# Scatters, masks, roots and zero fills rearranged, and an earlier shared expert, in an attention-plus-experts kernel

## The chip, the core and the metric

The kernel runs on one core of a Trainium2 chip. The metric is the device time of one launch in microseconds (us). Five engines run their own instruction queues in order: PE (matrix multiply; PEld is its weight load), DVE and ACT (elementwise work, ACT with function tables), POOL (elementwise work and indirect DMA) and SP (here only DMA issue). They wait for each other through semaphores. Sixteen DMA engines carry all transfers.

## What is computed

Sixteen sequences of 512 tokens, 128 wide, all float32. First a linear attention with a rotary-like expansion of q and k, then a mixture of experts, each followed by a layernorm:

```python
q, k, v = silu(x @ Wq), silu(x @ Wk), x @ Wv            # 16 heads of 8
q, k = lrpe(q, theta), lrpe(k, theta)                   # [t * cos(theta * n), t * sin(theta * n)]
out = ((q @ k.T) * causal) @ v                          # no softmax
out = (out @ Wo) * sigmoid(x @ G1 @ G2)
x = layernorm(x + layernorm(out) * gamma + beta)

xn = x * rsqrt(mean(x * x) + eps)
probs = softmax(xn @ router_w.T)                        # 8 experts, top 2 per token
dispatch, valid = first 1280 tokens of each expert, which of these slots are filled
routed = scatter_add(w * valid * (silu(x[dispatch] @ rg) * (x[dispatch] @ ru)) @ rd)
shared = (silu(x @ sg) * (x @ su)) @ sd                 # width 1024, for every token
x = layernorm(x + shared + routed)
```

## The kernel before

There are three stages. PE has work in all of them, and the order of PE, ACT, DVE and POOL is written out by hand (`tc.manual_schedule(engines=ORDERED)`, line 18 names the four). SP is not among these: the scheduler may place SP's DMA issues elsewhere than the program text has them, as soon as what they read is there.

**Attention, lines 177 to 780.** Work goes in turns `t` from -2 to 64, one tile of 128 tokens per turn, four tiles (`NC`) per sequence, in a pipeline: in turn `t` `project(t + 2)` computes q, k, v and the gate (`pq`, ACT evacuates it, DVE makes `hat` from it and the table `cst_tok` of cosines and sines), `turn_over(t + 1)` transposes, `energies(t)` multiplies q and k and DVE masks the result (`et`, four of 128x384), `values(t - 1)` multiplies with v (`pout`) and `remember` keeps a running state for the next tile. When a sequence's four tiles are done, the generator `after(b)` is appended to `turns`: output projection (`po`), two layernorms (`ln_stats`, `rstd_of`, `w`), the normalised rows `x1`, their transposes (`px`, `x1T`) and the router's logits. Each call of `advance(turns)` takes one of its steps, two calls per turn; a step that yields "narrow" waits for the call with that name. `route(b0, b1)` does top-2, the ranks of tokens in their expert and `count` per expert, some steps per turn (`sprinkle`). The resulting row numbers feed `scatter`: an indirect DMA on POOL that writes 128 token rows of `R` = 132 numbers into `xg_dram`, two per turn (`scatter_behind`, at the end of a turn), 128 in all.

**Shared expert.** Its steps for all sequences stand in one list, `feed`: per sequence eight `gate_half` (`pg`, L125) and eight `up_half` (`pu`, L133), then eight `down_half` (`pd`, L143). `shared(t)` takes one step where PE would have room: two per turn once the sequence is `ready`, one per turn of the loop that follows turn 64 (lines 780 to 797, which runs until the last scatter and twelve steps more), and what is left after the experts, where it covers the final layernorms.

**Experts, lines 800 to 951.** For each of eight experts the weights and the 1280 gathered rows `xg` (128 partitions x 10 x 132) are loaded, the rows transposed in three parts of 512, 512 and 256 (`turn_rows`: `ept`, copied to `xgT`), multiplied (`peg`, `peu`, `eh`, `ped`) and scattered by an indirect DMA into `y_dram`, two rows per token. The transposes of expert e+1 are done within expert e: after each `eh` of its second part first one `back` (`ped`), then one part of `turn_rows`.

**End, lines 953 to 983.** `load_pair` reads the two routed rows of each token back, `add_up` adds them, `finish_lot` does the last layernorm for lots of four tiles (single tiles for the last sequence) and stores them. A generator of these moves one step per step of `feed`.

Two fills belong to the change. `y_dram` must be zero where no expert writes a row; `zero` (128x2048) is written to it by eight DMAs of 1024 KB. Empty slots of `xg_dram` must be recognised; `empty`, with `NOBODY` as its token number, is written there by eight DMAs of 660 KB, before any scatter. `fill(t)` issues one per turn in turns 0 to 15.

At the start `cst_tok` is made from theta: broadcast to 128 partitions by its load (`th_sb`), multiplied by the positions, reduced by 2 pi in three steps (`C1`, `C2`, `C3`), then sines on ACT. Chunk 0 is done first and chunks 1 to 3 together, all before turn -2's `hat`. POOL clears the padded v tiles (`vpad`, `vlow`) and makes the masks and routing constants.

Of the kernel before, what the change touches and what calls it, by code (L numbers as in the profile page):

```python
# [10 lines left out]
F32 = mybir.dt.float32  # L11
I32 = mybir.dt.int32
# [7 lines left out]
P = 128  # L20
# [8 lines left out]
NOBODY = 1.0e6  # L29
# [6 lines left out]
C1 = 6.28125  # L36
C2 = 2029.0 / 2 ** 20
C3 = 2.0 * math.pi - C1 - C2
# [9 lines left out]
def tile_kernel(  # L48
# [37 lines left out]
    nc.gpsimd.memset(neghalf, -0.5)  # L86
    x1 = keep.tile([P, NT, R], F32, name="x1")
# [5 lines left out]
    idx = keep.tile([P, 2, NT], I32, name="idx")  # L93
    sg_sb = keep.tile([P, IS], F32, name="sg_sb")
# [10 lines left out]
    def rstd_of(var, n, eps):  # L105
        ve = small.tile([P, n], F32, tag="ve", name="ve")
        nc.vector.tensor_scalar(ve, var, eps, None, ALU.add)  # L107
        r = small.tile([P, n], F32, tag="rstd", name="rstd")
        nc.gpsimd.tensor_tensor(r, ve, neghalf[:, :n], ALU.pow)  # L109
        return r  # L110


    def shared_steps(b):
# [6 lines left out]
        def gate_half(i):  # L120
            if i % half == 0:
                h[i // half] = hp.tile([P, half, N], F32, tag="h", name=f"h_{b}_{i}")
            pool, tag = home["g"]
            pg = pool.tile([P, N], F32, tag=tag, name=f"pg_{b}_{i}")
            nc.tensor.matmul(pg, sg_sb[:, ts(i, P)], seq, start=True, stop=True)  # L125
            sl = sp.tile([P, N], F32, tag="sl", name=f"sl_{b}_{i}")
            nc.scalar.activation(sl, pg, AF.Silu)  # L127
            h["s", i] = sl

# [30 lines left out]
    done = set()  # L160
    latest = [None]
# [15 lines left out]
    with ExitStack() as ph:  # L177
# [21 lines left out]
        with tc.manual_schedule(engines=ORDERED):  # L199
            th_sb = cst.tile([P, D + HALF], F32, name="th_sb")  # L200
            nc.sync.dma_start(th_sb, theta.partition_broadcast(P))
# [3 lines left out]
            load_xT(0)  # L205
            g1t_sb = cst.tile([8, D], F32, name="g1t_sb")
            nc.scalar.dma_start(g1t_sb, g1t)
            g2_sb = cst.tile([8, D], F32, name="g2_sb")
            nc.scalar.dma_start(g2_sb, g2)
# [7 lines left out]
            nc.gpsimd.memset(rw_sb, 0.0)  # L217
# [3 lines left out]
            load_x(1)  # L221
# [3 lines left out]
            nc.sync.dma_start(bet, beta.partition_broadcast(P))  # L225

# [19 lines left out]
            expi = cst.tile([P, E], I32, name="expi")  # L246
            nc.gpsimd.iota(expi, pattern=[[1, E]], base=0, channel_multiplier=0)
            expf = cst.tile([P, E], F32, name="expf")
            nc.vector.tensor_copy(expf, expi)
            first = cst.tile([P, E], F32, name="first")  # L250
            nc.vector.tensor_scalar(first, expf, -1.0, float(E), ALU.mult, ALU.add)
            startrow = cst.tile([P, E], F32, name="startrow")
            nc.vector.tensor_scalar(startrow, expf, float(CAP), float(-NSLOT), ALU.mult, ALU.add)
            count = cst.tile([P, E], F32, name="count")
            nc.vector.memset(count, 0.0)
            goes_on = {}
            for n in sorted({(b1 - b0) * NC for b0, b1 in groups}):
                goes_on[n] = cst.tile([P, E, n + 1], F32, name=f"goes_on{n}")
                nc.gpsimd.memset(goes_on[n], 1.0)
                nc.gpsimd.memset(goes_on[n][:, :, 0], 0.0)  # L260


            ones = cst.tile([P, P], F32, name="ones")
            nc.vector.memset(ones, 1.0)

            causal = cst.tile([P, 3, HALF], F32, name="causal")
            nc.gpsimd.memset(causal, 1.0)
            for block, at in ((0, 0), (0, HALF), (1, HALF), (2, 0)):
                rows = causal[at : at + HALF, block, :]
                nc.gpsimd.affine_select(  # L270
                    rows, rows, pattern=[[1, HALF]], compare_op=ALU.is_ge, fill=0.0, base=0, channel_multiplier=-1
                )
            tri = cst.tile([P, P], F32, name="tri")
            nc.gpsimd.affine_select(
                tri, ones, pattern=[[1, P]], compare_op=ALU.is_gt, fill=0.0, base=0, channel_multiplier=-1
            )
# [7 lines left out]
            )  # L284


            NVP = 4
            vpads = []
            for i in range(NVP):
                vp = cst.tile([P, 4, 4, 40], F32, name=f"vpad{i}")  # L290
                nc.gpsimd.memset(vp, 0.0)

                vl = cst.tile([P, 8, 40], F32, name=f"vlow{i}")
                nc.gpsimd.memset(vl, 0.0)
                vpads.append((vp, vl))


            toki = cst.tile([P, NT], I32, name="toki")
            nc.gpsimd.iota(toki, pattern=[[P, NT]], base=0, channel_multiplier=1)
            zero = hp.tile([P, 4 * N], F32, tag="h", name="zero")  # L300
            nc.gpsimd.memset(zero, 0.0)
            empty = hp.tile([P, NS, R], F32, tag="h", name="empty")
            nc.gpsimd.memset(empty, 0.0)
            nc.gpsimd.memset(empty[:, :, D], NOBODY)


            pg = ps_w.tile([P, D], F32, tag="w", name="pg12")
            nc.tensor.matmul(pg, g1t_sb, g2_sb, start=True, stop=True)

            cst_tok = cst.tile([P, NC, 2, 16, 2, 8], F32, name="cst_tok")
            scratch = hp.tile([P, 2, NC, D + HALF], F32, tag="h", name="scratch")
            ang, turns_ = scratch[:, 0], scratch[:, 1]
            for c0, c1 in ((0, 1), (1, NC)):
                a, k = ang[:, c0:c1, :], turns_[:, c0:c1, :]
                for c in range(c0, c1):
                    nc.vector.tensor_scalar(ang[:, c, 0:D], th_sb[:, 0:D], pos[:, 0, c : c + 1], None, ALU.mult)
                    nc.vector.tensor_scalar(ang[:, c, D:], th_sb[:, D:], pos[:, 1, c : c + 1], None, ALU.mult)
                nc.vector.tensor_scalar(k, a, 1.0 / (2.0 * math.pi), MAGIC, ALU.mult, ALU.add)  # L320
                nc.vector.tensor_scalar(k, k, MAGIC, None, ALU.subtract)
                for part in (C1, C2, C3):
                    nc.vector.scalar_tensor_tensor(a, k, -part, a, ALU.mult, ALU.add)
                nc.vector.tensor_scalar(a, a, -PI_BELOW, PI_BELOW, ALU.max, ALU.min)
                nc.vector.scalar_tensor_tensor(k, a, -1.0, a, ALU.mult, ALU.max)

                for c in range(c0, c1):
                    for s, (from_, scale, bias) in enumerate([(turns_, -1.0, half_pi), (ang, 1.0, 0.0)]):
                        for to, n0, n1 in ((cst_tok[:, c, 0], 0, D), (cst_tok[:, c, 1, 1::2], D, D + HALF)):
                            nc.scalar.activation(  # L330
                                to[:, :, s, :], from_[:, c, n0:n1].rearrange("p (h d) -> p h d", d=8), AF.Sin,
                                scale=scale, bias=bias,
                            )
                if c0 == 0:
                    nc.vector.tensor_copy(  # L335
                        W[:, 0:384].rearrange("p (h n) -> p h n", n=24)[:, :, 8:16], pg.rearrange("p (h d) -> p h d", d=8)
                    )
            for c0, c1 in ((0, 1), (1, NC)):
                nc.vector.tensor_copy(
                    cst_tok[:, c0:c1, 1, 0::2].rearrange("p c h s d -> p c h (s d)"),  # L340
                    cst_tok[:, c0:c1, 0, 0::2].rearrange("p c h s d -> p c h (s d)"),
                )
            nc.vector.tensor_scalar(wo_sb, wo_sb, 0.5, None, ALU.mult)
            nc.vector.tensor_copy(x1[:, :, D], toki)


        y_rows = y_dram.rearrange("(p q r) d -> p q (r d)", p=P, r=4 * N // D)
        x_rows = xg_dram.rearrange("(p q r) d -> p q (r d)", p=P, r=NS)

        def fill(i):  # L350
            if i < 8:
                nc.sync.dma_start(y_rows[:, i, :], zero)
            elif i < 16:
                nc.sync.dma_start(x_rows[:, i - 8, :], empty.rearrange("p r d -> p (r d)"))

        hats, qkt, ets, states, gates, oTs = {}, {}, {}, {}, {}, {}


        def project(t):
# [22 lines left out]
            for i in range(2):  # L382
                mine = slice(HALF * i, HALF * i + HALF)
                nc.scalar.copy(vl[mine, :, 8 * i : 8 * i + 8], pq[mine, 8:16, 16 + 8 * i : 24 + 8 * i])
            hats[t] = hat = wk2.tile([P, 2, 2 * D], F32, tag="hat", name=f"hat_{t}")
# [350 lines left out]
        with tc.manual_schedule(engines=ORDERED):  # L736
            for t in range(-2, NT + 1):
                coming, here, left = 0 <= t + 2 < NT, 0 <= t < NT, 0 <= t - 1 < NT
                stopped("wait")
                if coming:  # L740
# [3 lines left out]
                    project(t + 2)  # L744
                if t == 2:
# [3 lines left out]
                if 0 <= t < 16:  # L749
                    fill(t)  # L750
# [5 lines left out]
                advance(turns)  # L756
# [272 lines left out]
```

## Time and profile before

| | |
|---|---|
| Median of 11 runs | 889.5 us (887.49 to 890.67, and one of 2649.25) |
| The profiled execution's own time | 889.07 us |
| Its span, first to last instruction | 887.4 us |
| PE busy in the span | 827.0 us (93%) |
| DVE, ACT, POOL busy | 556.5, 441.2, 345.1 us |
| Mean granted PE clock | 0.983 |
| DMA moved | 62.97 MB, of it 31.88 MB written to HBM |

The rest of the page is in 40 slices of 22.2 us, a digit is the busy share in tenths:

```profile
## 2 busy tenths in 40 slices
PE   2898999999989999998999999999999999999990
PEld 1576667666855866765666666777667676666670
DVE  7678788998888888978533343333333326875543
ACT  3767777677676767654322233333333333343332
POOL 4023222156755665477666413343333340110101
PEclk9999999999999999999999999999999999999995
DMA  8941111012111110000000422332211005631001
```

The first eighteen or so slices are attention, with DVE nearly as full as PE; the next five the loop that follows turn 64; the experts run from slice 24 to 33; the rest is the end. Times in the timeline are from the first instruction of the span. "Idle before" is the time an engine stood still before a group of instructions, and after the arrow stands what ended it.

### The profile page before, as it was taken

Reading aid. Unit: us, or ns where it says so; the run is one execution under the profiler, and the core shown is the slowest. Engines: PE = TensorE matmul, PEld = TensorE weight load, DVE = VectorE, ACT = ScalarE, POOL = GpSimd, SP = SyncE. Lnnn points to the kernel's source line nnn. Section 1 sums busy time; section 2 is a strip of 40 time slices with the busy share of each in tenths; the row PEclk is TensorE's granted clock in tenths of the full one; section 3 lists DMA queues with packets and bytes.
Section 4 is the critical chain, followed back from the end, with each engine's and each line's share of the span. In section 5 each row is a group of like instructions: output and inputs, shape, how many; then the busy total and the mean of one; then the engine's idle time right before and its main releaser. Section 6 shows DMA issues by size and latency. Waiting matters only on the chain.

```text
span 887.4 us, 24496 instructions
## 1 busy us (share of the span) xinstructions
PE 827.0 (93%) x9790; PEld 568.1 (64%) x9790; DVE 556.5 (63%) x1687; ACT 441.2 (50%) x1285; POOL 345.1 (39%) x455
## 2 busy tenths in 40 slices
PE   2898999999989999998999999999999999999990
PEld 1576667666855866765666666777667676666670
DVE  7678788998888888978533343333333326875543
ACT  3767777677676767654322233333333333343332
POOL 4023222156755665477666413343333340110101
PEclk9999999999999999999999999999999999999995
DMA  8941111012111110000000422332211005631001
GB/s 284 417 158 47 32 33 33 16 44 57 57 46 50 57 51 27 21 26 19 11 5 1 128 51 87 90 97 79 63 59 60 28 28 149 178 115 37 24 26 46
DMA packets 64338, 62.97 MB, mean 71 GB/s; under 512 B 6179, under 2 KB 55130, under 8 KB 63200
## 3 DMA queue, kind: packets, MB, share of 16 engines
q1 hardware_dynamic: 57392, 50.44, 17.9%
q0 software_dynamic: 6656, 10.69, 3.8%
q8 instruction: 77, 1.26, 0.6%
q14 instruction: 37, 0.30, 0.1%
q10 hardware_dynamic: 176, 0.27, 0.1%
HBM read 32.71 MB, written 31.88 MB: 73 GB/s over the span
## 4 chain that ended last, share of the span: by engine, by line
PE 72%; DVE 20%; ACT 4%; issue 2%; DMA 1%; POOL 0%; POOLq 0%; DVEq 0%; ACTq 0%
PE pd L143 11%; PE pg L125 10%; PE pu L133 10%; PE ped L856 8%; PE peg L940 8%; PE peu L942 8%; DVE et L451 6%; PE pq L363 3%; PE pe L444 3%; DVE st L101 2%; PE pt L399 2%; PE pout L486 2%; DVE hat L386 2%; ACT x L532 1%; DVE w L518 1%
## 5 line engine op out<-in xcount | busy, mean ns | idle before, releaser
L109 POOL TENSOR_TENSOR rstd<-ve,neghalf 128x4 f32<-128x4 f32 (+1 forms) x51 | 52.4, 1028 | 254.8 <-DVE ve L107 219.8
L671 POOL DMA_INDIRECT xg_dram<-x,idx x128 | 132.8, 1037 | 38.1 <-issue 32.3
L127 ACT ACTIVATE sl<-pg 128x512 f32<-128x512 f32 x128 | 76.2, 596 | 126.2 <-PE pg L125 125.3
L945 DVE TENSOR_TENSOR eh<-esl,peu 128x512 f32<-128x512 f32 (+1 forms) x96 | 57.5, 599 | 128.0 <-PE peu L942 128.0
L862 POOL DMA_INDIRECT y_dram<-y,to x80 | 77.6, 970 | 154.3 <-ACT y L860 154.3
L134 DVE TENSOR_TENSOR h<-sl,pu 128x512 f32<-128x512 f32 x128 | 87.7, 685 | 76.6 <-PE pu L133 64.4
L125 PE MATMUL pg<-x1T,sg_sb 128*128 128x512 f32 x256 | 131.9, 597 | 2.2 <-DVE h L134 0.9
L133 PE MATMUL pu<-x1T,su_sb 128*128 128x512 f32 x256 | 131.0, 593 | 0.5 <-ACT sl L127 0.5
L451 DVE TENSOR_TENSOR et<-pe,causal 128x384 f32<-128x384 f32 x256 | 124.6, 550 | 9.1 <-PE pe L444 8.9
L143 PEld LDWEIGHTS pd<-sd_sb,h 128*128 128x128 f32 x1024 | 118.7, 192 | 5.6 <-issue 5.0
L143 PE MATMUL pd<-sd_sb,h 128*128 128x128 f32 x1024 | 121.8, 275 | 0.0
L856 PEld LDWEIGHTS ped<-rd,eh 128*128 128x128 f32 x640 | 84.0, 192 | 24.6 <-issue 22.7
L940 PE MATMUL peg<-xgT,rg 128*128 128x512 f32 (+1 forms) x192 | 84.6, 522 | 0.0
L942 PE MATMUL peu<-xgT,ru 128*128 128x512 f32 (+1 forms) x192 | 84.4, 521 | 0.0
L856 PE MATMUL ped<-rd,eh 128*128 128x128 f32 x640 | 84.3, 275 | 0.0
L944 ACT ACTIVATE esl<-peg 128x512 f32<-128x512 f32 (+1 forms) x96 | 50.5, 526 | 55.9 <-PE peg L940 53.9
L133 PEld LDWEIGHTS pu<-x1T,su_sb 128*128 128x128 f32 x256 | 45.7, 190 | 45.5 <-issue 39.7
L860 ACT ACTIVATE y<-ped,wt 128x128 f32<-128x128 f32 x80 | 29.4, 368 | 84.6 <-PE ped L856 84.6
L125 PEld LDWEIGHTS pg<-x1T,sg_sb 128*128 128x128 f32 x256 | 44.3, 191 | 39.1 <-issue 33.9
L363 PE MATMUL pq<-W,xT 128*128 128x384 f32 x128 | 60.3, 554 | 7.6 <-DVE W L335 6.8
L444 PE MATMUL pe<-q,kT 32*64 32x192 f32 x2048 | 62.0, 336 | 0.7 <-issue 0.7
L386 DVE TENSOR_TENSOR hat<-qk,cst_tok 128x512 f32<-128x512 f32 x64 | 45.2, 706 | 22.3 <-ACT qk L371 22.1
(164 smaller groups left out, 1265.5 us busy)
## 6 DMA issues: line engine op xcount, KB each, us to landing
y_dram<-zero SPq DMA_DIRECT2D x8, 1024.0 KB, 11.0
y<-y_dram SPq DMA_DIRECT2D x32, 256.0 KB, 3.3
xT<-xt SPq DMA_DIRECT2D x16, 384.0 KB, 3.2
xg_dram<-empty SPq DMA_DIRECT2D x8, 660.0 KB, 14.8
xg<-xg_dram SPq DMA_DIRECT2D x8, 660.0 KB, 5.6
x<-x SPq DMA_DIRECT2D x16, 256.0 KB, 3.3
o<-res SPq DMA_DIRECT2D x15, 256.0 KB, 2.3
xg_dram<-x,idx POOLq DMA_INDIRECT x128, 2.3
```

The source lines that it names most:

```text
L125: nc.tensor.matmul(pg, sg_sb[:, ts(i, P)], seq, start=True, stop=True)
L133: nc.tensor.matmul(pu, su_sb[:, ts(i, P)], seq, start=True, stop=True)
L134: nc.vector.tensor_tensor(h[i // half][:, i % half, :], h.pop(("s", i)), pu, ALU.mult)
L143: nc.tensor.matmul(pd, h[k][:, i - k * half, ts(c, P)], sd_sb[:, i, :], start=(i == 0), stop=(i == IS // P - 1))
L363: nc.tensor.matmul(pq[:, :, 0:24], xts[b][:, c, 0:P], W[:, 0:384].rearrange("p (h n) -> p h n", n=24), start=True, stop=True)
L444: nc.tensor.matmul(pes[g][mine, s], kT[rows, s, mine], q2[rows, s, 3 * i : 3 * i + 3], start=(s == 0), stop=(s == 1),)
L451: nc.vector.tensor_tensor(et.rearrange("p s k n -> p s (k n)"), pes[g].rearrange("p s k n -> p s (k n)"), causal.rearrange("p k n -> p (k ...
L671: i = nc.gpsimd.indirect_dma_start(out=xg_dram[:, :], out_offset=bass.IndirectOffsetOnAxis(ap=idx[:, k, t : t + 1], axis=0), in_=x1[:, t, ...
L856: nc.tensor.matmul(pd, h[:, i, ts(c, P)], got[e][2][:, i, :], start=(i == 0), stop=(i == IR // P - 1))
L862: i = nc.gpsimd.indirect_dma_start(out=y_dram[:, :], out_offset=bass.IndirectOffsetOnAxis(ap=to[:, at : at + 1], axis=0), in_=y, in_offset ...
L940: nc.tensor.matmul(pg[:, :n], rg_sb[:, ts(i, P)], xgTs[e][:, ds(o0, n)], start=True, stop=True)
L942: nc.tensor.matmul(pu[:, :n], ru_sb[:, ts(i, P)], xgTs[e][:, ds(o0, n)], start=True, stop=True)
```

## The change

- *Start.* Theta is loaded as one row, broadcast by a matmul with ones (`pth`) and copied by ACT. Angles and sines are made chunk by chunk: chunks 0 and 1 at the start, chunk 2 in turn 0, chunk 3 in turn 1 (`beginning`). The reduction by 2 pi takes two steps instead of three and uses `turns_of`, computed once. Half of the padded v tiles are cleared by ACT (`nought`); POOL's masks wait for chunk 0. The routing constants move to turn 2 (`constants_of_routing`). `g1t` and `g2` are loaded on SP ahead of xT, whose first tile has a load of its own. The scaling of `wo_sb` moves to turn 0.
- *Fills.* `empty` and its eight DMAs are gone. `zero` is 128x256, cleared by ACT at the end of turn 1; `y_dram` is filled by sixteen DMAs of 512 KB that read it four times over, in rows of 1 KB. The program text issues them in the loop after turn 64, one every fourth step.
- *Masks.* `turn_rows` now zeroes the rows of empty slots itself: from `count` and the slot's number (`slotno`) it makes all-ones or zero (`ok[:, 0]`), and one `bitwise_and` per part is applied to `xg` before its transposes. `targets_of` adds `NOBODY` (now 2^20, an integer) to the targets of empty slots by a `bitwise_or`.
- *Scatters.* The two scatters of a turn stand ahead of `advance(turns, "narrow")` instead of behind `sprinkle(t, 4)`.
- *Double pace.* While `t < 8`, each `advance(turns)` is done twice; `ready[0]` is `t + 4` instead of `t + 10`, so that the first shared step is in turn 8 instead of 14.
- *Roots.* Once the last `gate_half` of the last sequence has been issued, ACT loads the table of square roots (`warm_root`), and the layernorms that follow take `Sqrt` on ACT and a reciprocal on DVE (`rstd_by_root`) instead of POOL's power.

```diff
-NOBODY = 1.0e6
+NOBODY = 1 << 20
...
-C1 = 6.28125
-C2 = 2029.0 / 2 ** 20
-C3 = 2.0 * math.pi - C1 - C2
+C1 = 102944.0 / 2 ** 14
+C2 = 2.0 * math.pi - C1
...
+    def rstd_by_root(var, n):
+        root = small.tile([P, n], F32, tag="ve", name="root")
+        nc.scalar.activation(root, var, AF.Sqrt, bias=eps_col)
+        r = small.tile([P, n], F32, tag="rstd", name="rstd")
+        nc.vector.reciprocal(r, root)
+        return r
...
+            if (b, i) == (B - 1, IS // P - 1):
+                warm_root = small.tile([P, 1], F32, tag="warm_root", name="warm_root")
+                nc.scalar.activation(warm_root, eps_col, AF.Sqrt)
+                roots.append(warm_root)
...
-            th_sb = cst.tile([P, D + HALF], F32, name="th_sb")
-            nc.sync.dma_start(th_sb, theta.partition_broadcast(P))
+            th_row = cst.tile([1, D + HALF], F32, name="th_row")
+            nc.sync.dma_start(th_row, theta.unsqueeze(0))
...
+            def nought(tile_, n):
+                nc.scalar.copy(tile_, zcol.to_broadcast([P, n]))
+            pth = ps_w.tile([P, D + HALF], F32, tag="w", name="pth")
+            nc.tensor.matmul(pth, ones[0:1, :], th_row, start=True, stop=True)
+            th_sb = cst.tile([P, D + HALF], F32, name="th_sb")
+            nc.scalar.copy(th_sb, pth)
...
+            for vp, vl in vpads[2:]:
+                nought(vp.rearrange("p a b d -> p (a b d)"), 640)
+                nought(vl.rearrange("p a d -> p (a d)"), 320)
...
+        def angles(c, th):
+            a, size, k, whole = scratch[:, c], scratch[:, NC + c], scratch[:, 8], scratch[:, 9]
+            both = ((slice(0, D), pos[:, 0, c : c + 1]), (slice(D, D + HALF), pos[:, 1, c : c + 1]))
+            for m, at in both:
+                nc.vector.tensor_scalar(k[:, m], turns_of[:, m], at, MAGIC, ALU.mult, ALU.add)
+            nc.vector.tensor_scalar(whole, k, MAGIC, -C1, ALU.subtract, ALU.mult)
+            for m, at in both:
+                nc.vector.scalar_tensor_tensor(a[:, m], th[:, m], at, whole[:, m], ALU.mult, ALU.add)
+            nc.vector.tensor_scalar(k, k, MAGIC, -C2, ALU.subtract, ALU.mult)
+            nc.vector.tensor_tensor(a, a, k, ALU.add)
+            nc.vector.scalar_tensor_tensor(size, a, -1.0, a, ALU.mult, ALU.max)
+            nc.vector.tensor_scalar(a, a, -PI_BELOW, PI_BELOW, ALU.max, ALU.min)
...
+            angles(0, pth)
+            sines(0)
+            angles(1, th_sb)
+            same(0)
...
+        def beginning(t):
+            if t == -1:
+                sines(1)
+            elif t == 0:
+                angles(2, th_sb)
+                sines(2)
+            elif t == 1:
+                angles(3, th_sb)
+                sines(3)
+        def beginning_done(t):
+            if t == 1:
+                nought(zero, N // 2)
+            elif t == 2:
+                constants_of_routing()
...
         def fill(i):
-            if i < 8:
-                nc.sync.dma_start(y_rows[:, i, :], zero)
-            elif i < 16:
-                nc.sync.dma_start(x_rows[:, i - 8, :], empty.rearrange("p r d -> p (r d)"))
+            nc.sync.dma_start(y_rows[i], zero.unsqueeze(1).to_broadcast([P, 4, N // 2]))
...
-                if 0 <= t < 16:
-                    fill(t)
...
-                advance(turns)
+                pace = 2 if t < 2 * NC else 1
+                for _ in range(pace):
+                    advance(turns)
...
-                    ready[b] = t + (6 if b else 10)
+                    ready[b] = t + (6 if b else 4)
...
+                if t % 4 == 1 and fills:
+                    fill(fills.pop(0))
...
+            if o0 == 0:
+                ok = ep.tile([P, 2, NS], I32, tag="ok", name=f"ok_{e}")
+                nc.vector.tensor_scalar(ok[:, 0], slotno, count[:, e : e + 1], -1.0, ALU.is_lt, ALU.mult)
+                nc.vector.tensor_scalar(ok[:, 1], slotno, count[:, e : e + 1], float(NOBODY), ALU.is_ge, ALU.mult)
+                taken[e] = ok
+            here = slice(o0 // P, (o0 + n) // P)
+            rows = xg[:, here, :].bitcast(I32)
+            nc.vector.tensor_tensor(
+                rows, rows, taken[e][:, 0, here].unsqueeze(2).to_broadcast([P, n // P, R]), ALU.bitwise_and
+            )
...
+            nc.vector.tensor_tensor(to, to, taken[e][:, 1], ALU.bitwise_or)
...
-            rs = rstd_of(mv[:, :, 1], n, LN_EPS)
+            rs = rstd_by_root(mv[:, :, 1], n) if roots else rstd_of(mv[:, :, 1], n, LN_EPS)
```

## The prediction

> **What bounds the kernel now.** I read the page's first two parts, then the busy time by stretch, then the chain of waits and the timeline where a stretch showed idle PE. Stretches (length, busy us of PE, PEld, DVE, ACT, POOL, then clock, DMA share, GB/s):
>
> ```profile
> 10.00:20.00 10.00, 3.69 (x8) 2.27 (x8) 9.55 (x22) 3.20 (x17) 2.09 (x3) 1.00 1.01 351
> ...
> 30.00:40.00 10.00, 7.53 (x209) 5.40 (x207) 6.00 (x13) 6.63 (x27) 0.45 (x1) 1.00 1.01 413
> 40.00:50.00 10.00, 8.02 (x145) 6.28 (x152) 3.92 (x8) 4.84 (x21) 1.67 (x2) 0.83 0.98 384
> ...
> 600.00:700.00 100.00, 100.00 (x521) 71.62 (x520) 36.51 (x77) 36.48 (x81) 35.88 (x37) 1.00 0.21 62
> ...
> 860.00:887.40 27.40, 5.59 (x51) 5.40 (x49) 7.76 (x43) 6.82 (x16) 5.20 (x7) 0.64 0.14 39
> ```
>
> PE is the bound: full in the experts (600 to 700 us), idle only at the start, in the turns under the zero fills (30 to 50) and in the last 22 us. All its work is in the changed kernel too, so the change is worth what it does to PE's idle time.
>
> Start, from the timeline: DVE computes angles until the first `hat` at 20.13, PE stands before `pq` until 14.21.
>
> ```profile
> 6.07 2.82 DVE L318 TENSOR_SCALAR scratch<-th_sb,pos 128x128 f32<-128x128 f32 x1 [2.83 <-DMA th_sb<-theta]
> ...
> 14.21 1.65 PE L363 MATMUL pq<-W,xT 128*128 128x384 f32 x2 [6.80 <-DVE W L335]
> ...
> 20.13 0.69 DVE L386 TENSOR_TENSOR hat<-qk,cst_tok 128x512 f32<-128x512 f32 x1
> ```
>
> Under the fills, from the chain of waits: three gaps in which PE waits for nothing that the profile shows, each just behind a 16 KB instruction transfer, with the DMA engines full; after the longest the clock drops and `pq` takes 1.58 us instead of 0.84.
>
> ```profile
> 32.05 0.69 issue
> ...
> 37.24 1.78 issue
> ...
> 43.03 1.98 issue
> ...
> 46.31 1.58 PE pq L363 x2
> ```
>
> In an expert, from the timeline, around a transpose of the next expert's rows: `ept` follows `ped` at once; DVE's `eh` begins 0.27 us after `ped` does.
>
> ```profile
> 547.05 1.05 PE L856 MATMUL ped<-rd,eh 128*128 128x128 f32 x8
> ...
> 547.32 0.69 DVE L945 TENSOR_TENSOR eh<-esl,peu 128x512 f32<-128x512 f32 x1 [1.03 <-PE peu L942]
> 547.83 0.47 PEld L833 LDWEIGHTS ept<-ident,xg 128*128 128x128 f32 x4
> ```
>
> **The change part by part.**
>
> *Start.* One 768 B row replaces the broadcast of theta that landed at 6.05. Indirect rows here land in 2.2 us, so about 2.8; the `ones` matmul 0.76 (row of `pg12`), ACT's copy 0.4 behind its table load: 4.1. DVE then has ten operations per chunk at 0.19 to 0.37 (the undisturbed chain at 12.1 to 13.9), 2.5 us: chunk 0 at 6.9, chunk 1 at 9.3. ACT clears two vpad pairs first (0.69 and 0.42 by the 0.587 of a 128x512 copy, 2.2 in all), so W is whole at 6.6 and `pq` of turns -2 and -1 starts there; 2.1 to its end (14.21 to 16.32 before), 1.1 for the copies, 0.88 for four sines, 0.2 and 0.7 for `same` and `hat`: first `hat` ends at 11.7 instead of 20.8. But chunks 2 and 3 now stand in turns 0 and 1, on DVE ahead of `hat` and `et`: second `hat` 12.8, state 13.7, angles 16.0, sines 16.8, `hat` 17.8, four `et` 19.8, angles 22.3, sines 23.0, `hat` 24.0; ACT's turn-over copies (1.8), oT and the clearing of `zero` reach 26.5, where `qk` of turn 2 starts; before 30.87. **-4.4** (bounds 0 to -9, if the later chunks eat all or nothing).
>
> *Fills.* The rows for `xg_dram` (8 x 660 KB) fall away. The 8 MB for `y_dram` stand in the program's last loop, but the SP queue is not one whose order is held, and in the changed program's order eleven of the sixteen stand right behind the load of xT of sequence 2, five behind sequence 3's: they start when ACT has cleared `zero`, about 27. So the attention turns are not rid of them. Rows are 1 KB instead of 8: the stretch of pure fills moves 426 GB/s, the stretch of 512 B rows (750 to 775 us: 4.48 MB at 62.4% of the engines) 287 when busy, so 8.4 MB take 20 to 29 us, 25 by the middle, instead of 33 for both fills. Fetches have to pass queued packets of about 0.05 us instead of 0.31, so I expect some of the gaps to go: the three gaps and the cold turn (about 1.9) are 6.3; I leave 2.3. Four small routing constants on DVE add 0.5. `qk` of turn 2 to that of turn 5: 17.4 before, three clean turns of 3.7 plus 2.8 after: **-3.5** (-6 to +2).
>
> The Trainium skill, "DMA: Bandwidth & Descriptors", Rules for kernel authors, asks for 1 MiB or more per transfer, and these become 512 KB; its Specifications give full rate from 512 B. The rows here already contradict the second (287 against 426 GB/s), and by it alone the fills would take 20 us and one gap more would go, some 1.5 us off the sum.
>
> *Double pace and shared steps from turn 8.* In turns 5 and 6 DVE gets `hat` 0.69, `et` 1.86, `add` 0.2 and half of the layernorm each: `o`, stats, `w` 2.9 in the one, `w`, stats, nb and sq 2.75 in the other: 5.7 and 5.5. Turn 7 has px, which waited for ACT in turn 9 before (px at 69.73): 5.3. Turns 8 to 13 then carry two shared steps each; turns 14 to 17 do that now in 22.76 us (89.68 to 112.44), 5.69 each: 34.1. Sum 50.6. Before, from the end of turn 5's `pq` (48.3) to that of turn 14's (90.8): 42.5. **+8.1** (+5 to +10). For it twelve steps leave the last stage, where a sequence's sixteen ups and eight downs take 20.88: 12 x 0.87 = **-10.4**; PE is full there, so all of it counts. The scatters now stand ahead of POOL's rstd and rms in a turn; rstd is read a turn later: 0 (-3 to +3, POOL works 63 of 100 us there).
>
> *Masks on the gathered rows.* This is the dear part. Per expert three `bitwise_and` on DVE, 528, 528 and 264 wide, each behind an `eh` in DVE's queue and ahead of the `ept` that PE does next; PE takes its queue in order. No integer row exists; nearest is the in-place sum of two f32 tiles in SBUF, the same shape:
>
> ```profile
> L889 DVE TENSOR_TENSOR x1T<-x1T,y x23: 291/684/689, 740.4 to 780.5; 128x512 f32<-128x512 f32 x22, 128x128 f32<-128x128 f32 x1
> ```
>
> So 0.70 us for 528 and 0.43 for 264 (the 128x256 `eh`). Counting from 547.32: `eh` holds DVE 0.60, the two small operations on `ok` 0.30, the mask 0.70, 0.1 to PE: `ept` at 549.0 instead of 547.83, 1.2 late. At the second part 0.60 + 0.70 + 0.1 from 550.37 against 550.88: 0.9. Third, 0.60 + 0.43 + 0.1 from 553.41 against 553.92: 0.6. PE has nothing else it may do: 2.7 per expert, seven times: **+18.9** (12.6 if the mask ran at twice that speed, 24 if POOL's descriptors slow it). Behind each late `ept` all of PE's queue is late; DVE, at 37% here, has room. For expert 0 the first mask lies under the last shared steps, but the next two alternate with the xgT copies of 0.69: 3.9 to the first `peg` against 1.66 (509.48 to 511.14), less 0.3 that the last step's shorter DVE work gives back: **+2.0** (+0.5 to +3). `to` gets one 0.17 operation, hidden behind `ped`.
>
> The skill's "TensorE: Matmul & The Clock Gate", Part 1, lets the clock fall after an idle window of about 3.4 us; here it fell after a gap of 1.98 and not after 1.78. By either, waits of 1.2 keep it.
>
> *Roots.* After the last matmul DVE and POOL alternate:
>
> ```profile
> 867.89 1.01 POOL L109 TENSOR_TENSOR rstd<-ve,neghalf 128x4 f32<-128x4 f32 x1 [6.08 <-DVE ve L107]
> ...
> 873.06 0.55 POOL L109 TENSOR_TENSOR rstd<-ve,neghalf 128x1 f32<-128x1 f32 x1 [0.97 <-DVE ve L107]
> ```
>
> A lot of four takes 3.19 now (869.01 to 872.20), a single 1.52. With ACT's root (0.2, the 128x1 activation) and DVE's reciprocal (0.2): 2.3 and 1.05. But twelve steps fewer of cover leave three lots of four behind the last matmul instead of two: 0.3 + 3 x 2.3 + 4 x 1.05 = 11.4 against 12.8. **-1.4** (-3 to +1). The table load (1.28) lies under the last downs.
>
> **Sum:** -4.4 - 3.5 + 8.1 - 10.4 + 18.9 + 2.0 - 1.4 = +9.3. The profiled execution took 889.07 (span 887.4), 0.4 under the median of 889.5: 889.07 + 9.3 = 898.4, said as **898**.
>
> **Rivals.** (a) *The masks cost PE nothing.* Place: `ept` behind `ped`. If they ran ahead of `eh`, or under 0.3 us, `ped`'s 0.89 would hide them: 889.07 - 11.6 = 877.5. For it: DVE is two thirds idle. Against: the order of its queue, and 0.684 for 512 f32. It decides for faster once the masks' waits are under about 1.3 us per expert. (b) *Fills hit harder.* Sixteen transfers of 1 KB rows keep the DMA engines full through turns 2 to 7 and the gaps come back and more: +6, 904. For it: all three gaps lie in full stretches; against: smaller packets, a third fewer bytes. (c) *Head and turns gain their bounds* (-9, -6, +5) and the masks their low one, 12.6: 889.07 - 9 - 6 + 5 - 10.4 + 12.6 + 0.5 - 1.4 = 880.4; half of that way gives no change, near 889.5. (d) *The fills do move to the end*: only if the recorded order were not the one run; nothing speaks for it.
>
> **Numbers.** Forecast 0.68 (891.5 to 903), (b) 0.12, (a) 0.07, (c) 0.05 with faster and 0.08 with no change. A difference under 0.2% (1.8 us) can't be told from none in this kernel. Faster 0.12, same 0.08, slower 0.80. The range, 889 to 905, takes in the upper bound of the masks, and leaves out the far ends of (a) and (c).
>
> **What would show it.** Right: `ept` groups with idle before them, released by DVE's mask, 2 to 3 us per expert, and PE's share from 600 to 700 near 0.9; first `pq` near 6.6; fills between about 27 and 52; the first `pg` of the shared expert in turn 8, and the last stage 10 us shorter. Wrong: `ept` without idle time (a), or PE gaps over 5 us from 27 to 52 (b).

## The result and the profile after

The changed kernel takes 903.67 us (median of 8 runs, 902.55 to 905.62), the kernel before 889.31 (31 runs); the ratio is 1.0163, with a 95% interval of 1.0152 to 1.0174. The profiled execution after has a span of 901.9 us and an own time of 903.6, against 887.4 and 889.07 before. So the change costs 14.4 us, 14.5 by the two spans.

The first view is the busy time by stretch, for the stretches shown of before (the last one counted from the end). Columns: length, busy us of PE, PEld, DVE, ACT and POOL with the number of instructions, then granted clock, DMA share, GB/s.

```profile
10.00:20.00 10.00, 7.21 (x148) 4.87 (x152) 8.34 (x27) 7.42 (x30) 0.52 (x1) 1.00 0.70 222
30.00:40.00 10.00, 9.82 (x303) 7.67 (x303) 8.06 (x17) 8.43 (x34) 1.69 (x2) 1.00 1.09 379
40.00:50.00 10.00, 6.33 (x132) 4.33 (x131) 9.07 (x40) 4.64 (x19) 3.27 (x4) 1.00 1.08 378
600.00:700.00 100.00, 93.73 (x480) 66.47 (x479) 39.05 (x91) 33.96 (x77) 33.24 (x35) 1.00 0.23 67
874.50:901.90 27.40, 11.17 (x74) 8.82 (x72) 13.24 (x63) 14.94 (x37) 0.00 (x0) 0.80 0.20 57
```

The fills still lie under the turns (DMA share above 1 from 30 to 50), but from 30 to 40 PE is now busy for 9.82 of 10 us instead of 7.53. From 40 to 50 it stands still more than before, in the experts, where it was always busy, it stands still for 6.3%, and POOL does nothing at the end.

Cutting both traces at the same events gives a table of where the time went. "Turn n" begins at the first `pq` of turn n or, where PE's queue has a semaphore record just ahead of it, at that record (0.75 us earlier at most); "last shared step" is the end of the last matmul of the shared expert ahead of the routed experts. By the `pq` matmuls alone the first four differences would be -6.4, -3.8, +12.8 and +3.0.

```
stretch                              before   after   difference  predicted
start to turn 2                       29.36   23.25      -6.1       -4.4
turn 2 to turn 5                      16.13   12.43      -3.7       -3.5
turn 5 to turn 14                     44.02   56.20     +12.2       +8.1
turn 14 to turn 61                   283.81  286.93      +3.1        0
turn 61 to the last shared step      135.26  136.97      +1.7        0
last shared step to first ped         11.25   16.43      +5.2       +2.0
first ped to last ped                210.75  228.93     +18.2      +18.9
last ped to last pd                  135.00  124.53     -10.5      -10.4
last pd to the end                    21.77   16.22      -5.6       -1.4
sum                                  887.36  901.89     +14.5       +9.3
```

Three readings of the timeline explain most of it. The first is the start: `pq` begins at 5.76 and the first `hat` at 10.18, where before they began at 14.21 and 20.13.

```profile
5.76 1.65 PE L419 MATMUL pq<-W,xT 128*128 128x384 f32 x2 [1.29 <-ACT W L294]
...
10.18 0.69 DVE L444 TENSOR_TENSOR hat<-qk,cst_tok 128x512 f32<-128x512 f32 x1
```

The second is turn 7, which begins at 44.49 and lasts 13.86 us; before it lasted 3.86.

```profile
42.63 0.91 PE L502 MATMUL pe<-q,kT 32*64 32x192 f32 x32
...
46.71 1.94 DVE L509 TENSOR_TENSOR et<-pe,causal 128x384 f32<-128x384 f32 x4
46.88 1.01 POOL L113 TENSOR_TENSOR rstd<-ve,neghalf 128x4 f32<-128x4 f32 x1 [2.88 <-DVE ve L111]
48.57 0.15 DVE L586 SCALAR_TENSOR_TENSOR nb<-mv,rstd 128x4 f32<-128x4 f32 x1
...
48.76 0.88 ACT L590 ACTIVATE x<-w,nb,rstd 128x128 f32<-128x128 f32 x2 [3.36 <-DVE nb L586]
...
49.30 0.71 PE L606 MATMUL px<-ident,x 128*128 128x128 f32 x2 [2.71 <-ACT x L590]
...
49.54 0.25 ACT L426 ACTIVATE qk<-pq 128x128 f32<-128x128 f32 x1
...
52.32 0.88 ACT L590 ACTIVATE x<-w,nb,rstd 128x128 f32<-128x128 f32 x2
...
52.87 0.86 PE L606 MATMUL px<-ident,x 128*128 128x128 f32 x2 [2.86 <-ACT x L590]
...
53.66 1.58 PE L502 MATMUL pe<-q,kT 32*64 32x192 f32 x32
```

The first line is from turn 6. Read on from the second. At double pace the two empty steps that gave `rstd` its time are used up at once, so `nb` stands directly behind `rstd` on POOL and four `et` on DVE. ACT's `x` is next in ACT's queue and waits 3.36 us for `nb`, while the `qk` copies of the turn, whose input is ready, stand behind it. Only after these copies comes the second pair of `x`, and PE, whose queue has all of `px` ahead of the next `pe`, waits 2.71 and 2.86 us. Then the clock is down: `pe` takes 1.58 us for what took 0.91 in the turn before.

The third is an expert, around a transpose of the next expert's rows.

```profile
562.23 0.69 DVE L1025 TENSOR_TENSOR eh<-esl,peu 128x512 f32<-128x512 f32 x1 [1.03 <-PE peu L1022]
562.83 0.23 DVE L900 TENSOR_SCALAR ok<-slotno,count 128x10 int32<-128x10 f32 x1
...
563.10 0.70 DVE L905 TENSOR_TENSOR xg<-xg,ok 128x528 int32<-128x528 int32 x1
...
563.87 0.42 PEld L910 LDWEIGHTS ept<-ident,xg 128*128 128x128 f32 x4 [1.05 <-ACT y L938]
```

The mask takes 0.70 us, as the row of the in-place sum had it, and `ept` starts when it is done. The releaser named is `y`, but that was done at 563.42 (begun at 563.05, 0.37 long); the mask ends last, at 563.80. The list of all waits of PE for `ept` (total us, times, longest) has the same two names; before, it held 1.3 us in all.

```profile
PE ept L910 <- DVE xg L905: 10.4, 16, 1.4
PE ept L910 <- ACT y L938: 5.4, 6, 0.9
```

### The profile page after: what moved, and what is told of

It reads as the page before. It is cut to its first block, busy times and chain, and to the rows that moved or that the text cites. A ratio compares the mean times of both kernels' runs of the same rounds, so it can differ in the third digit from the quotient of the medians.

```text
span 901.9 us, 24559 instructions
## 1 busy us (share of the span) xinstructions
PE 833.4 (92%) x9792; PEld 568.6 (63%) x9792; DVE 574.1 (64%) x1753; ACT 447.4 (50%) x1302; POOL 333.0 (37%) x442
## 5 line engine op out<-in xcount | busy, mean ns | idle before, releaser
L113 POOL TENSOR_TENSOR rstd<-ve,neghalf 128x4 f32<-128x4 f32 x43 | 45.9, 1067 | 181.1 <-DVE ve L111 170.4
```

## The experiments

All times are medians; ratios are to the kernel before on the same chip, and the changed kernel's is 1.0163. With e1 to e8 the kernel before took 889.4 to 889.7 us.

**e1: the masks ahead of `eh`.** Only the place of the mask in DVE's order differs, for experts 1 to 7.

```diff
+                        if o0 == parts[1][0] and e + 1 < E and i < len(parts):
+                            mask_rows(e + 1, *parts[i])
                         nc.vector.tensor_tensor(h[:, i, :n], sl[:, :n], pu[:, :n], ALU.mult)
                         for todo_ in (backs, aside):
```

> The masks of experts 1 to 7 stand ahead of the step's eh on VectorE instead of behind it; expert 0 and all else as in the changed kernel. Theory (the cost is the place in VectorE's queue): VectorE stands idle 1.03 us ahead of each eh in the trace, a mask takes 0.70, so ept follows ped at once, the ept waits on a mask go, and the time is 903.7 - 18 = 885 to 887. Rival (the work itself costs, by making eh late or by slowing VectorE): less than half of the 18 us comes back, 895 to 904.

Measured: 885.0 us, ratio 0.9951 (0.9937 to 0.9964). The timeline of this kernel, at the same place, and its busy time from 600 to 700:

```profile
561.37 0.70 DVE L903 TENSOR_TENSOR xg<-xg,ok 128x528 int32<-128x528 int32 x1
...
562.28 1.05 PE L938 MATMUL ped<-rd,eh 128*128 128x128 f32 x8
...
562.55 0.69 DVE L1032 TENSOR_TENSOR eh<-esl,peu 128x512 f32<-128x512 f32 x1 [0.48 <-PE peu L1027]
563.07 0.47 PEld L914 LDWEIGHTS ept<-ident,xg 128*128 128x128 f32 x4
```

```profile
600.00:700.00 100.00, 100.00 (x503) 69.75 (x502) 42.09 (x92) 36.83 (x81) 34.90 (x36) 1.00 0.24 74
```

The mask still takes 0.70, but lies in the time in which DVE waits for `peu`; `eh` begins 0.27 after `ped`, as before, and `ept` has no idle time ahead of it. First to last `ped` is 210.86 us, the 210.75 of before. The same 21 masks in another place cost 0.1 us: the whole price was their place in the queue.

**e2: expert 0's masks ahead of its transposes.**

```diff
-            for o0, n in parts:
-                turn_rows(0, o0, n)
+            mask_rows(0, *parts[0])
+            mask_rows(0, *parts[1])
+            turn_rows(0, *parts[0])
+            mask_rows(0, *parts[2])
+            turn_rows(0, *parts[1])
+            turn_rows(0, *parts[2])
```

> Only expert 0 differs from the changed kernel: two of its masks stand ahead of the first ept, the third ahead of the second, so that no mask stands between an xgT copy and the next ept. Theory: of the first expert's start (from the end of the last pd to the first peg 6.0 us instead of 2.67, then 1.9 us at half clock) the waits for the second and third mask go and with them the half clock: 3 to 4 us off, about 900. Rival: the start is late because the rows of expert 0 land late and the shared step's x1T stands behind a mask; then 0 to 1 us.

Measured: 903.0 us, ratio 1.0147 (1.0127 to 1.0166), two of the five runs at 900 and three at 903. In the profiled one (900.3) the stretch from the last shared step to the first `ped` is 13.66 us instead of 16.43: 2.8 of the 3 to 4 us that the theory expected, though the half clock only became shorter and did not go. The median is 0.6 us under that of the changed kernel, the rival's figure, so the time does not settle it. The remaining delay is the rival's: the first mask waited 2.25 us for the rows to land, and PE stood 1.93 us before the first `ept`, which needs the buffer that the last `x1T` frees, and that stood behind two masks. In e10 and e11 below, with two shared steps more ahead of the experts, the stretch is 11.6 and 11.3 us: before's 11.25 is reached, or nearly.

**e3: single pace in turn 7, and e9: `x` behind `qk`.** Two ways to take the stall of turn 7 apart; e3 shifts the end of the layernorm by half a turn, e9 puts one more empty step ahead of `nb`.

```diff
e3
-                pace = 2 if t < 2 * NC else 1
+                pace = 2 if t < 2 * NC - 1 else 1
e9
             yield
             yield
+            if b == 0:
+                yield
             nb = small.tile([P, NC], F32, tag="nb", name="nb")
```

> Double pace in turns 5 and 6 only, turn 7 at single pace. Theory (head of ScalarE's queue): turn 7 takes 13.9 us because ScalarE's first x of the layernorm waits 3.36 us for nb, and the turn's qk copies and the second x, then px on TensorE, stand behind it; with px moved one turn on, turns 7 and 8 together take 11 to 13 us instead of 19 and the time is 896 to 898. Rival (the zero fills keep turn 7 slow, by instruction fetches or by holding back loads): turn 7 stays above 11 us, 902 to 904.

> The changed kernel, in which the first sequence's layernorm waits one step longer ahead of nb, so that its four x stand behind turn 7's qk copies in ScalarE's queue and px stands at the end of turn 7. Theory: turn 7's 13.9 us are the two waits of ScalarE for nb (3.4 us) and of TensorE for px behind the second pair of x (2.9 us) with the waits that follow; they go, turns 7 and 8 take 12 to 14 us together instead of 19.2, and the time is 897 to 899. Rival (VectorE has too much in turns 5 to 7 whatever the order): turns 7 and 8 stay at 16 us or more, as in the run with single pace in turn 7 (15.8), 900 to 902.

e3: 900.3 us, ratio 1.0128 (1.0112 to 1.0145); turn 7 takes 8.94 us and turn 8 6.84. The time falls, so the fills are not what holds turn 7, but less than forecast: `nb` is still where it was, and ACT's first `x` still waits 3.52 us for it. In e9 ACT copies `qk` first and makes all four `x` in one go:

```profile
48.19 0.28 ACT L426 ACTIVATE qk<-pq 128x128 f32<-128x128 f32 x1 [0.27 <-PE pq L422]
...
51.65 0.15 DVE L588 SCALAR_TENSOR_TENSOR nb<-mv,rstd 128x4 f32<-128x4 f32 x1
51.84 1.65 ACT L592 ACTIVATE x<-w,nb,rstd 128x128 f32<-128x128 f32 x4
...
54.15 1.12 PE L608 MATMUL px<-ident,x 128*128 128x128 f32 x4
```

Turns 7 and 8 together take 13.3 us instead of 19.2, within the 12 to 14 expected, and turn 5 to turn 14 is 51.1 us instead of 56.2. The time of e9, 904.2 us (ratio 0.9976, 0.9958 to 0.9995), can't be set beside the others: e9 to e11 ran on a chip on which the kernel before took 906.9 us, and e12 on one on which it took 909.1. Their traces are used, and their comparisons with each other. In e9 the gain of 5.1 us is followed by a loss of 5.2 between turn 14 and the last shared step, where its code is that of the changed kernel; e10 and e11 show a surplus of the same kind there. Some 2.5 us of it are eight waits of PE ahead of `pout` for which the trace names no releaser, where the changed kernel's trace has none; why that chip is slower in this stretch stays open.

**e4: a late GpSimd operation, and e7: the roots alone.** In the kernel before, 8 us lie between the last `res` and the end. The records of the trace below (start, length in ns, engine, instruction) show what fills them; the page counts a drain as no work.

```
before  877.59 8990 GpSimd DRAIN        880.76 7 Sync DRAIN       886.63 17 GpSimd EVENT_SEMAPHORE
after   872.68 9455 GpSimd DRAIN        901.12 7 Sync DRAIN       901.15 17 GpSimd EVENT_SEMAPHORE
```

All engines meet at the end of the program, and GpSimd comes only when its own last drain is done, 8.42 us after the end of its last operation. Before, that operation is the `rstd` of the very last lot, at 877.62, and the drain is the last thing to end, 5.9 us after SP was ready. With the roots on ACT, GpSimd's last operation is at 872.70 and the drain is over long before the end. e4 adds to the changed kernel one 128x1 operation on GpSimd that reads the last `nb` and whose result goes nowhere:

```diff
             nc.vector.scalar_tensor_tensor(nb, mv[:, :, 0], -1.0, rs, ALU.mult, ALU.mult)
+            if lot[1] == NT:
+                late = small.tile([P, 1], F32, tag="late", name="late")
+                nc.gpsimd.tensor_tensor(late, nb, neghalf[:, 0:1], ALU.mult)
```

> One GpSimd operation of 128x1 is added that reads the last nb; its result is not used. Theory: the program ends only when GpSimd's closing drain is done, which takes 9.0 us (before) and 9.5 (after) and is hidden in the changed kernel because GpSimd is done at 873.7; held back to the last nb it ends at about 908.3, and the time is 903.7 + 6.5 = 910. Rival: the 8 us between the last res and the end of the kernel before belong to its last store or to the profile; then the operation lies beside ScalarE's last res and nothing changes, 903 to 905.

e7 is the kernel before with `eps_col`, `rstd_by_root` and the early table load (`warm_root`) of the change, and their use:

```diff
-            rs = rstd_of(mv[:, :, 1], n, LN_EPS)
-            yield True
+            rs = rstd_by_root(mv[:, :, 1], n) if roots else rstd_of(mv[:, :, 1], n, LN_EPS)
             yield True
+            if not roots:
+                yield True
```

> The kernel before with nothing but the square root on ScalarE for the last layernorms. Theory (the program's end waits for GpSimd's closing drain, 9.0 us from the last GpSimd operation): with GpSimd out of the last lots the drain is hidden, so 889.5 - 5.9 = 883.6, less 1 to 3 for the shorter chain: 881 to 884. By the prediction's sizing, which counted the chain alone: -1.4 to -3.5, 886 to 888.

e4: 911.7 us, ratio 1.0253 (1.0239 to 1.0267): an operation of 0.19 us costs 8. In the profiled run, the fastest of five, it is 5.1: there 22.59 us lie behind the last `pd` instead of 16.22, the 6.4 that the drain explains, and 1.3 are gained elsewhere. The other four runs are some 3 us slower still, and that no trace explains. The drain runs from 897.54 for 8.65 us, and the closing barrier follows at 906.24. e7: 882.0 us, ratio 0.9926 (0.9909 to 0.9943): 7.4 us faster than before, with 13.92 us from the last `pd` to the end instead of 21.77. Both agree with the drain: in e7 the last `res` comes 2.0 us earlier behind the last `pd`, and the other 5.9 of the 7.8 us gained there lie behind it. The time lies outside what the prediction's sizing gave.

**e5: single pace, shared steps from turn 14 again.**

```diff
-                pace = 2 if t < 2 * NC else 1
+                pace = 1
...
-                    ready[b] = t + (6 if b else 4)
+                    ready[b] = t + (6 if b else 10)
```

> The changed kernel with the first sequence's layernorm at single pace and its shared steps from turn 14, as before. By the two traces the double pace costs 12.2 us from turn 5 to turn 14 and brings 10.5 in the last stage, so without it 903.7 - 1.7 = 902 (900 to 904), with a last stage that is 10 us longer. By the prediction's terms (+8.1 and -10.4) it would be 906.

Measured: 895.9 us, ratio 1.0074 (1.0052 to 1.0097): faster than both expectations. So the double pace, as built, costs 7.8 us. By the traces: 12.4 in turns 5 to 14 (56.20 against 43.82), 2.8 in turns 14 to 61 (286.93 against 284.15), 1.1 at the first expert and 2.4 behind the last `pd` (16.22 against 13.86), against the 10.5 of the last stage. The end was left out of the expectation: twelve steps fewer leave three lots of four behind the last matmul instead of two.

**e6: the scatters behind the layernorm steps again, and e8: the fills late.**

```diff
e6
-                if left:
-
-                    scatter_behind(oTs[(t - 1) // NC][:, ds((t - 1) % NC * P, 1)])
-                    scatter_behind()
                 advance(turns, "narrow")
...
                 sprinkle(t, 4)
+                if left:
+
+                    scatter_behind(oTs[(t - 1) // NC][:, ds((t - 1) % NC * P, 1)])
+                    scatter_behind()
e8
                 beginning_done(t)
+                if t == 22:
+                    nought(zero, N // 2)
```

(e8 also leaves out the clearing of `zero` in turn 1.)

> The changed kernel with the scatters behind the layernorm steps again, as before. Theory: the 3.1 us that turns 14 to 61 lose come from the scatters standing ahead of GpSimd's rstd and rms; undone, 900.5 to 901.5, and the turns 25 and 49 are back at 7.2 to 7.6 us from 9.0 and 9.5. Rival (the shifted phase of the work, or something else in these turns): 903 to 904.5.

> The tile of zeros is cleared in turn 22 instead of turn 1, so the sixteen fills lie in turns 23 and later. Theory: turn 7 does not hang on the fills and stays at 12 to 14 us; turns 2 to 6 lose 0 to 3 us, and the later turns gain some of it back: 901 to 905. Rival (b of the prediction, fills that hit harder): turns 2 to 7 get 6 us or more shorter.

e6: 903.2 us, ratio 1.0162 (1.0144 to 1.0181), no difference. Turn 49 came back only to 8.08 us, turn 25 not at all (9.53), and what its trace gains in turns 14 to 61 (284.84, 2.1 less) it loses around them; as an account of the time the theory falls. Single pace (e5), with the scatters where the change puts them, brings these two turns to 7.55 and 7.47 and the stretch to 284.15, and there the gain stays. So the later loss needs the shifted phase of the work that double pace leaves behind; what share the scatters have in it stays open. e8: 904.1 us, ratio 1.0165 (1.0147 to 1.0182), no difference either; turn 7 takes 15.1 us with no fill under it. Rival (b) falls, as the waits of PE from 27 to 52 in the changed kernel say already (total us, times, longest):

```profile
PE px L606 <- ACT x L590: 2.7, 1, 2.7
PE pout L544 <- issue: 0.8, 2, 0.6
PE pt L457 <- issue: 0.3, 1, 0.3
```

**e10, e11 and e12: what was learnt, together.** e10 is the changed kernel with single pace (e5), the masks ahead (e1), expert 0's masks as in e2, and two shared steps more ahead of the experts; e11 is the same with double pace and the `x` behind `qk` (e9); e12 is e10 again. Beside the edits above:

```diff
-            t, over, waited = NT + 1, 12, 0
+            t, over, waited = NT + 1, 14, 0
```

> All that was learnt, with single pace: masks ahead of eh, expert 0's first two masks together and two shared steps more ahead of it, first sequence as before. If the parts add up: 903.7 - 18.6 (masks) - 7.8 (pace) - 1 to 3 (first expert) = 874 to 876. If the pace and the masks share a gain, 878 or more.

> The same with double pace and the x behind qk. If the double pace is sound once turn 7 does not stall, it beats the single pace by some 3 us (10.5 in the last stage against 7 to 8 in the turns): 871 to 873. If its cost lies in the turns from 8 on as well, it stays behind: 877 to 881.

> The kernel of e10 once more, because the chip of e9 to e11 ran the kernel before in 906.9 us instead of 889.5. If the parts add up on a chip like the others: 895.9 (e5) - 18.2 (masks) - 3.7 (from the last shared step to the first ped: 15.3 us in e5, 11.6 in e10) = 874, ratio 0.980 to 0.985. If the chip of e9 to e11 was slow for the kernel before alone, 879 to 881 and a ratio of 0.989.

e10: 879.9 us, ratio 0.9709 (0.9683 to 0.9735). e11: 880.7, ratio 0.9727 (0.9699 to 0.9754). e12: 882.3, ratio 0.9697 (0.9668 to 0.9726), on a chip as slow for the kernel before as that of e10. Both versions beat the kernel before by 2.7 to 3.0% there; the changed kernel itself was not run on these chips, only e9 (904.2). On the other chips that total was not measured: e12 was meant to and did not meet one, and what adds up in microseconds stays open; the fastest measured there are e7 (882.0) and e1 (885.0). Between e10 and e11 nothing can be told, against the 3 us expected: double pace without the stall brings 10.5 us from the last `ped` to the last `pd` (122.74 against 133.28) and loses 6.4 from turn 5 to 14 (49.27 against 42.90), 1.7 from turn 14 to 61 and 2.3 behind the last `pd`.

## Why the prediction was right, and where it was not

**The masks: right in mechanism, place and size.** 18.9 was forecast and 18.2 measured from first to last `ped`; e1 shows that it is the wait behind `eh` in DVE's queue. Rival (a) named the cure, "if they ran ahead of `eh`", and e1 is that case.

**The fills: right.** -3.5 against -3.7, with the fills where the prediction put them, issued from 25.5 to 45.8; their packets run from 26.4 to 51.9, the 25 us of the forecast's middle. I left 2.3 us of gaps; the waits above hold 1.1 that no release explains. That the smaller packets removed the gaps is argued: no run has the 8 KB rows in the changed kernel.

**The start: right, too small** by 1.7. W was whole at 5.70 instead of 6.6, and the first `hat` done at 10.87 instead of 11.7; the later chunks cost less than counted.

**Double pace: the step that failed.** "Turn 7 has px, which waited for ACT in turn 9 before (px at 69.73): 5.3" was 13.86. The sum counted what each engine has to do in a turn and forgot what stands behind what: an operation on ACT that waits for a chain of DVE and POOL holds up the copies behind it, and these hold up PE. Turns 5 and 6 (8.8 instead of 11.2) and turns 8 to 13 (33.5 instead of 34.1) were near. Turn 7 alone is 8.6 over; the other turns (-3.0) and a count of before that was 1.5 short (42.5 against 44.02) hide half of it, so the net is 12.2 instead of 8.1. The last stage was right, 10.5 against 10.4. Together -2.3 was predicted for the pace, and 7.8 measured (e5), 2.8 of them in turns 14 to 61, which the prediction did not let it touch.

**The scatter order: right at nothing for the total** (e6), though turns 14 to 61 lost 3.1, which single pace takes back for the most part (e5). The 1.7 between turn 61 and the last shared step, also put at nothing, no run explains.

**The first expert: mis-sized**, 5.2 instead of 2.0. Of its parts, I had the masks that alternate with the `xgT` copies, but neither the wait of `x1T` behind the first mask nor the clock:

```profile
515.21 0.71 DVE L905 TENSOR_TENSOR xg<-xg,ok 128x528 int32<-128x528 int32 x1 [2.13 <-DMA xg<-xg_dram]
...
516.98 0.63 PE L910 MATMUL ept<-ident,xg 128*128 128x128 f32 x4 [1.20 <-DVE x1T L165]
...
518.25 0.70 DVE L905 TENSOR_TENSOR xg<-xg,ok 128x528 int32<-128x528 int32 x1
519.00 0.72 PEld L910 LDWEIGHTS ept<-ident,xg 128*128 128x128 f32 x4 [1.63 <-DVE xg L905]
519.00 1.12 PE L910 MATMUL ept<-ident,xg 128*128 128x128 f32 x4 [1.40 <-DVE xg L905]
...
521.79 1.91 PE L1020 MATMUL peg<-xgT,rg 128*128 128x512 f32 x2
```

**The end: mis-sized**, -5.6 instead of -1.4. The chain itself gained nothing: 13.3 us from the end of the last `pd` to that of the last `res` before, 13.7 after. With two lots of four behind the last `pd`, in e7 and e5, it is 11.35, so the roots save 2.0 and the third lot takes 2.35 back. The 5.9 us are GpSimd's drain, which the page doesn't count and the prediction didn't see. The tail of before, from the last `res` at 878.93 to a span of 887.4, was there to be asked about.

**The sum: in part luck.** Costs put too low (pace 4.1, first expert 3.2, later turns 4.8: 12.1 us) and gains put too low or costs put too high (start 1.7, end 4.2, masks 0.7, the rest 0.3: 6.9 us) leave 5.2 us. They half cancel, and that is why 903.7 lies in the range of 889 to 905 and not far above it. It lies just above the 891.5 to 903 that had most of the chance, at the 904 of rival (b), but not for the reason of (b), which e8 rules out.

## What to carry to other kernels

An operation costs what stands behind it: the same 21 masks, of 0.70 us at most, cost 18 us behind `eh` and 0.1 ahead of it, so before an operation is added to a queue, look for the engine's idle time and put the operation there. When steps are run at a faster pace, look at what the empty steps were for: here they covered the way from DVE over POOL back to ACT, and without them the head of ACT's queue stopped PE. Ask what the last microseconds of a span are, also when no engine is busy in them, and let the engine with the longest closing drain finish first.

## What the hardware did that was not expected

- GpSimd's drain at the end of the program lasts until 8.42 us after the end of its last operation, in the traces of before, after, e4 and e7 alike, whether that operation took 0.19, 0.54 or 1.01 us.
- The clock falls without a long wait. The prediction took it that waits of 1.2 us keep it. In the changed kernel two of 1.20 and 1.40 us, with four transposes of 0.63 us in all between them, were enough: from 519.0 on the next four take 1.12 us, and the granted clock is 0.50 afterwards:

```profile
521.70:525.20 3.50, 3.50 (x6) 1.44 (x5) 1.19 (x7) 0.60 (x1) 0.00 (x0) 0.50 0.22 38
```

What the runs have in common is the time from the end of the last shared step to the first `peg`, in which PE does nothing but wait and transpose. Where it is 2.67 (before), 2.98 (e10) or 2.67 us (e11), the first `peg` runs at full speed (0.595 us for one matmul); where it is 4.23 (e2), 5.04 (e5) or 6.00 us (after), at half (up to 1.06); the granted clock stands at half for 3.41 us in e2 and e5 and for 6.83 in the changed kernel. The Trainium skill, "TensorE: Matmul & The Clock Gate", Part 1, has the clock decided over windows of about 3.4 us that run freely, and Part 4 says that transposes do not count as busy in the same way. The two lengths, 3.41 and twice that, agree with Part 1; the rows do not contradict Part 4, but no run here tells what transposes do from what waits do. The prediction had taken Part 1 for a rule on single waits. A window that runs freely would also let e2 fall into two groups 3 us apart, but that the runs do not show.
